# Summing over partitions in squares: attention denominators by VectorE's transposes instead of TensorE's products with ones

## The chip, the cores and the metric

The kernel runs on one core of a Trainium2 chip. A core has TensorE (PE: matrix products, from SBUF into PSUM), VectorE (DVE), ScalarE (ACT), GpSimd (POOL) and DMA queues; each engine works through its own instructions in order and waits for the others by semaphores. The metric is device time in microseconds, the median of several runs; less is better. Before the change it is 3609.92 us (three runs, 3609.66 to 3611.45).

## The reference

Four images of 64x64 pixels with 256 channels, float32. Two layers, one after the other.

```python
# layer 0: attention of every pixel over all 4096 pixels of its image
q = x @ Wq + bq ; k = x @ Wk + bk ; v = x @ Wv + bv       # 32, 32 and 256 wide
attn = softmax(q k^T, axis=-1)
x = gamma * (attn @ v) + x
# layer 1: 3x3 depthwise convolution to 768, two pointwise layers, local attention
hid = gelu(conv3x3(x) @ w_up1 + b_up1)                    # 512 wide
h = x + hid @ w_up2 + b_up2
q, k, v = split(h @ w_qkv + b_qkv)
w = softmax(q . k over the 3x3 window / 16)               # zero-padded borders
out = h + sum over the window of w * v
```

Both softmaxes are computed without a shift: exponentials are summed, and the result is multiplied by the reciprocal of the sum. The change is about these two sums, the denominators.

## The kernel before

An image is cut into 8 blocks of 512 pixels, so there are 32 slots, one for each block. Slot s does the attention of layer 0 for block s and, interleaved with it, the stages of layer 1 for earlier blocks: `hidden`, `update`, `guide` and `scores` for block s-3, `local_product` for block s-5. A slot has 16 points. At each point TensorE gets an energy (every second point), one job of the list, and a `product` that adds to the accumulators `acc`:

```python
jobs = [
    job(hidden, k, 0) + job(hidden, k, 1), job(local_denominator, a),
    job(hidden, k, 2), job(local_product, a, 0), job(hidden, k, 3),
    ...  # cut: update, guide, scores, local_sum (point 12), local_values (13 and 14)
]
...  # cut
    for point in range(points):
        G, half = divmod(point, 2)
        after = slot + (G + 1) // NG, (G + 1) % NG
        if half == 0:
            if G == NG // 2 and slot + 1 < NSLOT:
                spread_queries(slot + 1)

            if G == NG // 2:
                for do in job(border, k - 1):
                    do()
            if after[0] < NSLOT:
                energy(*after)
        if after[0] < NSLOT:
            weight(*after, half)
        for do in jobs[point]:
            do()
        product(slot, G, half)

        if point == 0:
            add_up(slot, 0, 0)
        if point < points - 1:
            add_up(slot, *divmod(point + 1, 2))

        while stepped < min(n_steps, -(-(point + 1) * n_steps // (points - 2))):
            next(conv, None)
            stepped += 1
    ...  # cut: loads
...
if slot < NSLOT - 1:
    next(finish(slot))
```

The exponentials `p` have keys on the 128 partitions and pixels (queries) on 512 columns. VectorE adds them up in `den`; what is left is a sum over partitions:

```python
def add_up(s, G, half):

    p = weights[s, G, half]
    if G == 0 and half == 0:
        sums[s] = tile_of([P, 2, NB], "den", f"den_{s}")
        nc.vector.tensor_copy(sums[s], p)
        return
    den = sums[s]
    nc.vector.tensor_tensor(den, den, p, ALU.add)
    if G == NG - 1 and half == 1:
        nc.vector.tensor_tensor(den[:, 0, :], den[:, 0, :], den[:, 1, :], ALU.add)
```

`finish` sums `den` over partitions by a product with a matrix of ones. Where there is a local denominator `lsums[a]` of an earlier block (slots 4 to 30, "shared"), the two are summed side by side in halves of 64 columns of the array; one reciprocal serves both, and copies spread the halves over 128 partitions:

```python
def finish(s, parts=((0, RB),)):

    g = s % NBLK
    den, acc = sums.pop(s), accs.pop(s)

    dps = bank("m", f"dps_{s}")
    rden = tile_of([P, NB], "rden", f"rden_{s}", 2)
    a = s - LAG_ATT + 1


    shared = 0 <= a < DIRECT - 1
    if shared:
        for half, weights_ in zip(halves, (den[:, 0, :], lsums.pop(a))):
            nc.tensor.matmul(
                dps[half], lhsT=ones[:, : P // 2], rhs=weights_, start=True, stop=True
            )
        lrdens[a] = tile_of([P, CH, NB], "xc", f"turned_{s}", 2)[:, 0, :]
    else:
        nc.tensor.matmul(dps, lhsT=ones, rhs=den[:, 0, :], start=True, stop=True)
    os = [tile_of([P, NB], "o", f"o_{s}_{c}", 3) for c in range(CH)]
    for r0, r1 in parts:
        n = slice(r0 * W, r1 * W)
        nc.vector.reciprocal((lrdens[a] if shared else rden)[:, n], dps[:, n])
        if shared:
            for half in halves:
                nc.vector.tensor_copy(rden[half], lrdens[a][halves[0]])
        for c, o in enumerate(os):
            nc.vector.scalar_tensor_tensor(
                o[:, n], acc[c][:, n], gam[:, 0:1], rden[:, n], ALU.mult, ALU.mult
            )
        for c, o in enumerate(os):
            dst = xv[:, c, 1 + g * RB + r0 : 1 + g * RB + r1, 1 : 1 + W]
            nc.vector.tensor_tensor(
                dst, o[:, n].rearrange("p (h w) -> p h w", w=W), dst, ALU.add
            )
        if r1 < RB:
            yield
    watch(den[:, 0, :])
    if len(parts) > 1:
        yield
    watch(rden)
    for o in os:
        watch(o)
    yield

def local_denominator(s):
    turned, lrdens[s] = lrdens[s], tile_of([P, NB], "rden", f"lrden_{s}", 2)
    for half in halves:
        nc.scalar.copy(lrdens[s][half], turned[halves[1]])
    watch(lrdens[s])
```

The local denominator's tile is summed by GpSimd, and in the last blocks by TensorE directly:

```python
def local_sum(s):


    t = tile_of([P, NB], "lsum", f"lsum_{s}")
    tv = t.rearrange("p (h w) -> p h w", w=W)
    nc.gpsimd.memset(t, 0.0)
    for half in range(2):
        for (block, t_), rows, of in pieces(s):
            to = tv[:, rows, columns(half)]
            nc.gpsimd.tensor_tensor(to, to, near_ws[block, half][:, t_, of, :], ALU.add)
    one = t[0:1, :].rearrange("p (h w) -> p h w", w=W)
    edge = one[:, :, 0 : W : W - 1]
    nc.gpsimd.tensor_tensor(edge, edge, pad_side[0:1], ALU.add)
    row = edge_row(s)
    if row is not None:
        nc.gpsimd.tensor_tensor(one[:, row, :], one[:, row, :], pad_line[0:1], ALU.add)
    watch(t)
    lsums[s] = t
...  # cut
def local_reciprocal(s):
    lrdens[s] = tile_of([P, NB], "rden", f"lrden_{s}", 2)
    nc.vector.reciprocal(lrdens[s], totals.pop(s))
    watch(lrdens[s])
```

`watch(values)` adds a tile into `watched` on GpSimd, so that at the end an overflow can be seen (`good`, `bad`); a second, shifted version of the whole kernel then runs. It does not run with these inputs. PSUM has 8 banks: 4 for the energies `e`, 2 for `acc`, 2 under the name "m" for all jobs and for `dps`.

Of the kernel before, what the change touches and what calls it, by code (L numbers as in the profile page):

```python
# [9 lines left out]
F32 = mybir.dt.float32  # L10
AF = mybir.ActivationFunctionType
ALU = mybir.AluOpType
AX = mybir.AxisListType
PSUM = bass.MemoryType.PSUM

P = 128
B, H, W, C = 4, 64, 64, 256
N = H * W
CQK = C // 8
CH = C // P  # L20
HP, WP = H + 2, W + 2
NB = 512
RB = NB // W
# [12 lines left out]
NEG = -1.0e30  # L36
GRP = P // CQK
NG = NT // GRP
NSLOT = B * NBLK


# [3 lines left out]
LAG_PERC, LAG_HID, LAG_ATT = 2, 3, 5  # L45
# [3 lines left out]
def attention_then_perception_kernel(  # L49
# [19 lines left out]
    nc = tc.nc  # L69

    const = ctx.enter_context(tc.tile_pool(name="const", bufs=1))
# [4 lines left out]
        return t  # L76

    ones = const.tile([P, P], F32, tag="ones", name="ones")
    watched = const.tile([P, NB], F32, tag="watched", name="watched")
    bad = const.tile([P, 1], mybir.dt.int32, tag="bad", name="bad")  # L80


# [1 line left out]
    def unshifted():  # L84
# [6 lines left out]
        def tile_of(shape, tag, name, bufs=1):  # L91
            return pool.tile(shape, F32, tag=tag, name=name, bufs=bufs)

        def bank(tag, name):
            return psum.tile([P, NB], F32, tag=tag, name=name, bufs=2)
# [46 lines left out]
        for r in range(KR):  # L142
            m = near[r * KW : (r + 1) * KW]
# [9 lines left out]
                if abs(q - 1 - r) > 1:  # L153
                    nc.gpsimd.memset(m[:, :, q, :], 0.0)

        ident = pool.tile([P, P], F32, tag="ident", name="ident")
        make_identity(nc, ident)

        def watch(values):

            nc.gpsimd.tensor_tensor(watched, watched, values, ALU.add)  # L161


        queries, keys, values, staged = {}, {}, {}, {}
# [94 lines left out]


        energies, weights, sums, accs, lsums, lrdens = {}, {}, {}, {}, {}, {}
        halves = slice(0, P // 2), slice(P // 2, P)

        DIRECT = NSLOT - LAG_HID - 1

# [31 lines left out]
        def add_up(s, G, half):  # L297
# [8 lines left out]
            if G == NG - 1 and half == 1:  # L306
                nc.vector.tensor_tensor(den[:, 0, :], den[:, 0, :], den[:, 1, :], ALU.add)  # L307

        def finish(s, parts=((0, RB),)):

            g = s % NBLK
            den, acc = sums.pop(s), accs.pop(s)

            dps = bank("m", f"dps_{s}")
            rden = tile_of([P, NB], "rden", f"rden_{s}", 2)
            a = s - LAG_ATT + 1


            shared = 0 <= a < DIRECT - 1
            if shared:  # L320
                for half, weights_ in zip(halves, (den[:, 0, :], lsums.pop(a))):
                    nc.tensor.matmul(  # L322
                        dps[half], lhsT=ones[:, : P // 2], rhs=weights_, start=True, stop=True
                    )
                lrdens[a] = tile_of([P, CH, NB], "xc", f"turned_{s}", 2)[:, 0, :]
            else:
                nc.tensor.matmul(dps, lhsT=ones, rhs=den[:, 0, :], start=True, stop=True)
            os = [tile_of([P, NB], "o", f"o_{s}_{c}", 3) for c in range(CH)]
            for r0, r1 in parts:
                n = slice(r0 * W, r1 * W)  # L330
                nc.vector.reciprocal((lrdens[a] if shared else rden)[:, n], dps[:, n])  # L331
                if shared:
                    for half in halves:
                        nc.vector.tensor_copy(rden[half], lrdens[a][halves[0]])
                for c, o in enumerate(os):
                    nc.vector.scalar_tensor_tensor(
                        o[:, n], acc[c][:, n], gam[:, 0:1], rden[:, n], ALU.mult, ALU.mult
                    )
                for c, o in enumerate(os):
                    dst = xv[:, c, 1 + g * RB + r0 : 1 + g * RB + r1, 1 : 1 + W]  # L340
                    nc.vector.tensor_tensor(
                        dst, o[:, n].rearrange("p (h w) -> p h w", w=W), dst, ALU.add
                    )
                if r1 < RB:
                    yield
            watch(den[:, 0, :])
            if len(parts) > 1:
                yield
            watch(rden)
            for o in os:  # L350
                watch(o)
            yield

        def local_denominator(s):
            turned, lrdens[s] = lrdens[s], tile_of([P, NB], "rden", f"lrden_{s}", 2)
            for half in halves:
                nc.scalar.copy(lrdens[s][half], turned[halves[1]])
            watch(lrdens[s])


        percs, hids, hs = {}, {}, {}
# [219 lines left out]
        def local_values(s, t):  # L581
            ps = job_bank(f"lv_{s}_{t}")
            for half in range(2):
                for kin in range(CH):
                    nc.tensor.matmul(  # L585
                        ps[:, half * C : (half + 1) * C],
                        lhsT=keys_of(s, t, half, kin), rhs=wlv[:, kin, :],
                        start=(kin == 0), stop=(kin == CH - 1),
                    )
            for half in range(2):  # L590
                if s < NSLOT - 2:
                    lvs[s, t, half] = tile_of([P, C], "lv", f"lv_{s}_{t}_{half}", 8)
                else:
                    if not half:
                        late[s, t] = tile_of([P, NB], "perc", f"lv_{s}_{t}", NPERC)
                    lvs[s, t, half] = late[s, t][:, half * C : (half + 1) * C]
                lv = lvs[s, t, half]
                nc.vector.tensor_tensor(lv, ps[:, half * C : (half + 1) * C], blv, ALU.add)  # L598
                if s >= NSLOT - 1:

                    square = tile_of([P, 2, NB], "den", f"lv_{s}_{t}_{half}_2")[:, 0, :C]
                    nc.gpsimd.tensor_tensor(square, lv, lv, ALU.mult)
                    nc.gpsimd.tensor_tensor(watched[:, :C], watched[:, :C], square, ALU.add)

        def pieces(s):

# [9 lines left out]
        def scores(s, half):  # L616


            g = s % NBLK
            ps = job_bank(f"s_{s}_{half}")  # L620

            tiles, rows, top = (2, QR, 0) if s < NSLOT else (1, UP, RB)
            n = tiles * rows * QW
            for t in range(tiles):
                for kin in range(CH):
                    nc.tensor.matmul(  # L626
                        ps[:, t * QR * QW : t * QR * QW + rows * QW].rearrange(
                            "p (h w) -> p h w", w=QW
                        ),
                        lhsT=keys_of(s, t, half, kin),  # L630
                        rhs=guides[0][:, kin, top + t * KR : top + t * KR + rows, columns(half)],
                        start=(kin == 0), stop=(kin == CH - 1),
                    )
            if s < NSLOT - 2:
                p = tile_of([P, 2 * QR * QW], f"lp{half}", f"lp_{s}_{half}", 2)
            else:

                if s < NSLOT:
                    late[s] = tile_of([P, NB], "perc", f"lp_{s}_{half}", NPERC)
                elif not half:  # L640
                    late[s] = tile_of([P, NB], "lsum", f"lp_{s}")
                p = late[s][:, : 2 * QR * QW]
                if s == NSLOT:
                    p = late[s][:, half * C : half * C + QR * QW]
            near_ws[s, half] = p.rearrange("p (t h w) -> p t h w", h=QR, w=QW)
            nc.scalar.activation(p[:, :n], ps[:, :n], AF.Exp, scale=C**-0.5)  # L646
            engine = nc.vector if s >= NSLOT - 2 else nc.gpsimd
            pv = p[:, :n].rearrange("p (t n) -> p t n", t=tiles)
            mask = near[:, half, :rows, :].rearrange("p h w -> p (h w)")
            engine.tensor_tensor(  # L650
                pv, pv, mask.unsqueeze(1).to_broadcast([P, tiles, rows * QW]), ALU.mult
            )

            if g == 0:
                nc.gpsimd.memset(p[P // 2 :, : UP * QW], 0.0)
                if s < NSLOT:
                    nc.gpsimd.memset(p[: P // 2, UP * QW : QR * QW], 0.0)
            if s >= DIRECT:

                nc.gpsimd.tensor_tensor(watched[:, :n], watched[:, :n], p[:, :n], ALU.add)  # L660

        def local_sum(s):

# [11 lines left out]
            row = edge_row(s)  # L675
            if row is not None:
                nc.gpsimd.tensor_tensor(one[:, row, :], one[:, row, :], pad_line[0:1], ALU.add)
            watch(t)
            lsums[s] = t

        def local_total(s):
# [18 lines left out]
                )  # L700

        def local_reciprocal(s):
            lrdens[s] = tile_of([P, NB], "rden", f"lrden_{s}", 2)
            nc.vector.reciprocal(lrdens[s], totals.pop(s))  # L704
            watch(lrdens[s])

        def local_product(s, c):
            b, g = divmod(s, NBLK)
# [58 lines left out]
        for slot in range(NSLOT):  # L767
# [44 lines left out]
            for point in range(points):  # L812
# [18 lines left out]
                    add_up(slot, 0, 0)  # L831
                if point < points - 1:
                    add_up(slot, *divmod(point + 1, 2))

                while stepped < min(n_steps, -(-(point + 1) * n_steps // (points - 2))):
                    next(conv, None)
# [481 lines left out]
```

## Time and profile before

| | |
|---|---|
| time | 3609.92 us (3609.66 to 3611.45) |
| span of the profiled execution | 3607.3 us |
| TensorE busy | 3579.5 us, 99% |
| VectorE busy | 2377.5 us, 66% |
| ScalarE busy | 1145.5 us, 32% |
| GpSimd busy | 705.9 us, 20% |
| granted TensorE clock, mean | 0.998 |

A page of the profile lists the busy time of each engine, the chain of work that ended last, and the costliest groups of instructions. A line of a group reads: source line, engine, operation, the tiles written and read, shapes, count, then busy time, the mean duration of one in ns, and the idle time of the engine before it with what ended it. A float32 product appears as two records, one for each pass; durations of products overlap, because they are pipelined, so starts tell more than durations. A line of a timeline has the start, the time taken by the merged instructions, the engine, the source line and the operation; a bracket gives the idle time before it and what released it.

The operations that the change removes or makes smaller, by group:

| operation | count | busy us | mean ns |
|---|---|---|---|
| VectorE reciprocal of 128x512 (shared) | 27 | 90.7 | 3358 |
| VectorE reciprocal of 128x512 (slots 0 to 3) | 4 | 13.4 | 3358 |
| VectorE reciprocal of 128x512 (local, last blocks) | 5 | 16.8 | 3354 |
| VectorE copy of 64x512 | 54 | 22.7 | 420 |
| ScalarE copy of 64x512 | 54 | 33.3 | 616 |
| GpSimd watch of den | 32 | 40.6 | 1268 |
| GpSimd watch of rden | 32 | 40.7 | 1273 |
| GpSimd watch of lrden | 32 | 50.3 | 1572 |
| GpSimd watch of lsum | 28 | 36.9 | 1319 |

### The profile page before, as it was taken

How to read it: one execution, taken by the hardware profiler on the slowest of the kernel's cores; microseconds unless marked ns; L12 is line 12 of the kernel's file. 1: busy time of each engine (PE TensorE's matmuls, PEld its weight loads, DVE VectorE, ACT ScalarE, POOL GpSimd, SP SyncE). 2: the span in 40 equal slices, each digit the busy share in tenths (PEclk: the TensorE clock that was granted, in tenths of full speed). 3: DMA queues.
4: the chain of work that ended last, by engine and by line, in shares of the span. 5: the costliest groups of instructions: out<-in, count | busy, mean ns of one | idle time of the engine just before them, and what ended most of it. 6: DMA issues, size and time to landing. Idle time of an engine off the chain costs nothing.

```text
span 3607.3 us, 29497 instructions
## 1 busy us (share of the span) xinstructions
PE 3579.5 (99%) x11400; PEld 1696.9 (47%) x11400; DVE 2377.5 (66%) x2742; ACT 1145.5 (32%) x1324; POOL 705.9 (20%) x720
## 2 busy tenths in 40 slices
PE   9999999999999999999999999999999999999998
PEld 4444444454444444455444444444544444444445
DVE  3376676657666667765666666675667766666976
ACT  2223333323333333332333333333233333333431
POOL 1010112111221222121112222112112122221224
PEclk9999999999999999999999999999999999999999
DMA  3000000010000000011000000001100000000000
GB/s 104 6 3 4 0 9 15 23 39 21 15 7 9 15 15 15 21 24 44 15 15 15 3 12 15 15 21 35 33 15 15 15 15 3 12 15 15 6 6 25
DMA packets 84532, 64.68 MB, mean 18 GB/s; under 512 B 57280, under 2 KB 62528, under 8 KB 84256
## 3 DMA queue, kind: packets, MB, share of 16 engines
q1 hardware_dynamic: 83568, 62.19, 5.9%
q8 instruction: 91, 1.49, 0.2%
q10 hardware_dynamic: 816, 0.53, 0.0%
q14 instruction: 57, 0.47, 0.0%
HBM read 41.52 MB, written 18.81 MB: 17 GB/s over the span
## 4 chain that ended last, share of the span: by engine, by line
PE 97%; DVE 3%; issue 0%; ACT 0%; DMA 0%; POOL 0%; SPq 0%; ACTq 0%; DVEq 0%
PE acc L291 48%; PE hid L424 18%; PE e L272 7%; PE dx L450 6%; PE v L235 3%; PE lv L585 3%; PE g L533 3%; PE lo L713 2%; PE s L626 2%; DVE perc L397 2%; PE qk L201 1%; PE dps L322 1%; PE c L565 0%; DVE den L305 0%; DVE rden L331 0%; DVE lrden L704 0%
## 5 line engine op out<-in xcount | busy, mean ns | idle before, releaser
L291 PE MATMUL acc<-p,v 128*128 128x512 f32 x4096 | 1837.4, 595 | 0.1
L397 DVE SCALAR_TENSOR_TENSOR perc<-xp,wperc,perc 128x512 f32<-128x512 f32 (+1 forms) x1554 | 1298.0, 836 | 430.2 <-ACT perc L393 395.0
L291 PEld LDWEIGHTS acc<-p,v 128*128 128x128 f32 x4096 | 769.5, 190 | 917.8 <-issue 913.9
L280 ACT ACTIVATE p<-e 128x1024 f32<-128x1024 f32 x512 | 524.3, 1024 | 1469.8 <-PE e L272 832.0
L424 PE MATMUL hid<-perc,wup 128*128 128x512 f32 x1536 | 686.1, 599 | 1.0 <-DVE perc L397 1.0
L305 DVE TENSOR_TENSOR den<-den,p 128x1024 f32<-128x1024 f32 x480 | 604.1, 1259 | 44.3 <-ACT p L280 40.6
L424 PEld LDWEIGHTS hid<-perc,wup 128*128 128x128 f32 x1536 | 284.7, 190 | 390.5 <-issue 377.6
L272 PE MATMUL e<-qa,ka 32*128 32x512 f32 x2048 | 291.9, 640 | 0.0
L161 POOL TENSOR_TENSOR watched<-watched,lo 128x512 f32<-128x512 f32 x62 | 127.1, 2049 | 670.5 <-DVE lo L720 670.3
L450 PE MATMUL dx<-hid,wup 128*128 128x512 f32 x512 | 233.0, 598 | 0.0
L428 ACT ACTIVATE hid<-hid,bup 128x512 f32<-128x512 f32 x128 | 88.0, 687 | 436.7 <-PE hid L424 436.7
L650 POOL TENSOR_TENSOR lp<-lp,near 128x396 f32<-128x396 f32 x60 | 57.8, 963 | 715.9 <-ACT lp L646 715.9
L598 DVE TENSOR_TENSOR lv<-lv,blv 128x256 f32<-128x256 f32 x130 | 49.1, 419 | 193.6 <-PE lv L585 193.6
L331 DVE RECIPROCAL turned<-dps 128x512 f32<-128x512 f32 x27 | 90.7, 3358 | 128.2 <-PE dps L322 128.2
L272 PEld LDWEIGHTS e<-qa,ka 32*128 32x128 f32 x2048 | 80.0, 182 | 171.7 <-issue 168.4
L456 DVE SCALAR_TENSOR_TENSOR h<-dx,bup,xp 128x256 f32<-128x256 f32 x128 | 56.0, 479 | 158.7 <-PE dx L450 158.7
L450 PEld LDWEIGHTS dx<-hid,wup 128*128 128x128 f32 x512 | 94.6, 190 | 129.9 <-issue 123.2
L393 ACT ACTIVATE perc<-xp,bperc,wperc 128x512 f32<-128x512 f32 x192 | 153.8, 803 | 5.2 <-PE hid L424 5.2
L280 ACT ACT_TABLE_LOAD x91 | 116.8, 1283 | 120.0 <-issue 119.4
L585 PE MATMUL lv<-wlv,h 128*128 128x256 f32 x520 | 126.5, 385 | 1.6 <-DVE lv L598 0.9
L161 POOL TENSOR_TENSOR watched<-watched,den 128x512 f32<-128x512 f32 x32 | 40.6, 1268 | 431.4 <-DVE den L307 431.4
L235 PE MATMUL v<-wv,xc 128*128 128x256 f32 x512 | 118.4, 384 | 6.1 <-DMA wv<-in_w_v 5.3
(105 smaller groups left out, 2064.0 us busy)
## 6 DMA issues: line engine op xcount, KB each, us to landing
xp<-in_x SPq DMA_DIRECT2D x30, 528.0 KB, 4.0
out<-lo SPq DMA_DIRECT2D x58, 256.0 KB, 2.0
xc<-in_x SPq DMA_DIRECT2D x48, 256.0 KB, 3.3
qa<-packed SPq DMA_DIRECT2D x124, 64.0 KB, 2.0
ka<-st SPq DMA_DIRECT2D x124, 16.0 KB, 1.8
packed<-st SPq DMA_DIRECT2D x31, 64.0 KB, 1.9
wup<-in_w_up SPq DMA_DIRECT2D x1, 1536.0 KB, 7.1
out<-res SPq DMA_DIRECT2D x6, 256.0 KB, 2.0
```

The costliest lines, as they stand in the source:

```text
L161: nc.gpsimd.tensor_tensor(watched, watched, values, ALU.add)
L235: nc.tensor.matmul(ps[:, i * C : (i + 1) * C], lhsT=xc[:, kin, bass.ts(2 * pair + i, P)], rhs=wv[:, kin, :], start=(kin == 0), stop=(kin = ...
L272: nc.tensor.matmul(e[:, j, :], lhsT=key[rows, :], rhs=queries[s][rows, :], start=True, stop=True,)
L280: nc.scalar.activation(p, energies[s, G][:, 2 * half : 2 * half + 2, :], AF.Exp)
L291: nc.tensor.matmul(accs[s][c], lhsT=v[:, 2 * half + i, bass.ts(c, P)], rhs=p[:, i, :], start=(first and i == 0), stop=(G == NG - 1 and hal ...
L305: nc.vector.tensor_tensor(den, den, p, ALU.add)
L393: nc.scalar.activation(acc, win, AF.Identity, bias=bperc[:, half, j : j + 1], scale=wt)
L397: nc.vector.scalar_tensor_tensor(acc, win, wt, acc, ALU.mult, ALU.add)
L424: nc.tensor.matmul(ps, lhsT=wup1[:, i, bass.ts(d, P)], rhs=percs[s][i], start=(i == 0), stop=(i == NPC - 1),)
L450: nc.tensor.matmul(ps, lhsT=wup2[:, d, bass.ts(c, P)], rhs=hids[s][:, d, :], start=(d == 0), stop=(d == NHC - 1),)
L533: nc.tensor.matmul(ps, lhsT=wg[:, kin, bass.ts(i, P)], rhs=pixels(s, kin), start=(kin == 0), stop=(kin == CH - 1),)
L585: nc.tensor.matmul(ps[:, half * C : (half + 1) * C], lhsT=keys_of(s, t, half, kin), rhs=wlv[:, kin, :], start=(kin == 0), stop=(kin == CH ...
```

## The change

The sum over 128 partitions is split in two steps. VectorE transposes each 32x32 square of the 128x512 tile, so that pixels come to lie on partitions within a square, and sums each square's 32 columns: 16 columns are left, with four groups of 32 partitions still to be added. TensorE adds these with the matrix `fold` (ones where two partitions agree modulo 32) in one product of 16 columns, or 32 for two denominators. The reciprocal is then taken of 16 or 32 columns; a spreading copy and another transpose of squares bring it back to 512 columns on all partitions. The aim is to take the sums off TensorE and to shorten the reciprocals.

The squares are summed at the slot's last point (`partial_sums`), before `finish`. The copies for the local denominator go from ScalarE to VectorE. `watched` has 256 columns, longer tiles are added in pieces, and the small tiles are watched in place of the large ones.

```diff
@@ -36,6 +36,8 @@
 NEG = -1.0e30
 GRP = P // CQK
 NG = NT // GRP
+SQ = 32
+NJ = NB // SQ
 NSLOT = B * NBLK
 
 
@@ -76,7 +78,7 @@
         return t
 
     ones = const.tile([P, P], F32, tag="ones", name="ones")
-    watched = const.tile([P, NB], F32, tag="watched", name="watched")
+    watched = const.tile([P, C], F32, tag="watched", name="watched")
     bad = const.tile([P, 1], mybir.dt.int32, tag="bad", name="bad")
 
 
@@ -153,12 +155,25 @@
                 if abs(q - 1 - r) > 1:
                     nc.gpsimd.memset(m[:, :, q, :], 0.0)
 
-        ident = pool.tile([P, P], F32, tag="ident", name="ident")
+        ident = tile_of([P, NB], "lsum", "ident")[:, :P]
         make_identity(nc, ident)
 
+
+        fold = pool.tile([P, P], F32, tag="fold", name="fold")
+        nc.gpsimd.memset(fold, 0.0)
+        for q in range(0, P, SQ):
+            part = fold[q : q + SQ].rearrange("p (j r) -> p j r", r=SQ)
+            nc.gpsimd.affine_select(
+                out=part, in_=part, compare_op=ALU.not_equal, fill=1.0,
+                base=0, pattern=[[0, P // SQ], [-1, SQ]], channel_multiplier=1,
+            )
+
         def watch(values):
 
-            nc.gpsimd.tensor_tensor(watched, watched, values, ALU.add)
+            n = values.free_size()
+            for i in range(0, n, C):
+                at = watched[:, : min(C, n - i)]
+                nc.gpsimd.tensor_tensor(at, at, values[:, i : min(n, i + C)], ALU.add)
 
 
         queries, keys, values, staged = {}, {}, {}, {}
@@ -259,7 +274,7 @@
 
 
         energies, weights, sums, accs, lsums, lrdens = {}, {}, {}, {}, {}, {}
-        halves = slice(0, P // 2), slice(P // 2, P)
+        parts_, inverses, turneds = {}, {}, {}
 
         DIRECT = NSLOT - LAG_HID - 1
 
@@ -306,32 +321,53 @@
             if G == NG - 1 and half == 1:
                 nc.vector.tensor_tensor(den[:, 0, :], den[:, 0, :], den[:, 1, :], ALU.add)
 
+        def squares(t):
+            return t.rearrange("p (j r) -> p j r", r=SQ)
+
+        def shared(s):
+
+            a = s - LAG_ATT + 1
+            return a if 0 <= a < DIRECT - 1 else None
+
+        def partial_sums(s):
+
+
+            a = shared(s)
+            parts_[s] = tile_of([P, 2, NJ], "parts", f"parts_{s}")
+            turneds[s] = tile_of([P, CH, NB], "xc", f"turned_{s}", 2)
+            todo = [sums[s][:, 0, :]] + ([] if a is None else [lsums.pop(a)])
+            for i, t in enumerate(todo):
+                nc.vector.transpose(turneds[s][:, i, :], t)
+                nc.vector.tensor_reduce(
+                    parts_[s][:, i, :], squares(turneds[s][:, i, :]), axis=AX.X, op=ALU.add
+                )
+            watch(parts_[s][:, : len(todo), :].rearrange("p i j -> p (i j)"))
+
+        def on_all(values, turned, out):
+
+            nc.vector.tensor_copy(
+                squares(turned), values.unsqueeze(2).to_broadcast([P, NJ, SQ])
+            )
+            nc.vector.transpose(out, turned)
+
         def finish(s, parts=((0, RB),)):
 
             g = s % NBLK
-            den, acc = sums.pop(s), accs.pop(s)
-
-            dps = bank("m", f"dps_{s}")
+            acc = accs.pop(s)
+            n = NJ * (1 if shared(s) is None else 2)
+            ps = bank("m", f"dps_{s}")[:, :n]
+            given = parts_.pop(s).rearrange("p i j -> p (i j)")[:, :n]
+            nc.tensor.matmul(ps, lhsT=fold, rhs=given, start=True, stop=True)
+            inverse = tile_of([P, 2, NJ], "inverse", f"inverse_{s}")
+            inverses[s] = inverse
+            nc.vector.reciprocal(inverse.rearrange("p i j -> p (i j)")[:, :n], ps)
             rden = tile_of([P, NB], "rden", f"rden_{s}", 2)
-            a = s - LAG_ATT + 1
-
-
-            shared = 0 <= a < DIRECT - 1
-            if shared:
-                for half, weights_ in zip(halves, (den[:, 0, :], lsums.pop(a))):
-                    nc.tensor.matmul(
-                        dps[half], lhsT=ones[:, : P // 2], rhs=weights_, start=True, stop=True
-                    )
-                lrdens[a] = tile_of([P, CH, NB], "xc", f"turned_{s}", 2)[:, 0, :]
-            else:
-                nc.tensor.matmul(dps, lhsT=ones, rhs=den[:, 0, :], start=True, stop=True)
+            on_all(inverse[:, 0, :], turneds[s][:, 0, :], rden)
+            watch(inverse.rearrange("p i j -> p (i j)")[:, :n])
+            sums.pop(s)
             os = [tile_of([P, NB], "o", f"o_{s}_{c}", 3) for c in range(CH)]
             for r0, r1 in parts:
                 n = slice(r0 * W, r1 * W)
-                nc.vector.reciprocal((lrdens[a] if shared else rden)[:, n], dps[:, n])
-                if shared:
-                    for half in halves:
-                        nc.vector.tensor_copy(rden[half], lrdens[a][halves[0]])
                 for c, o in enumerate(os):
                     nc.vector.scalar_tensor_tensor(
                         o[:, n], acc[c][:, n], gam[:, 0:1], rden[:, n], ALU.mult, ALU.mult
@@ -341,21 +377,16 @@
                     nc.vector.tensor_tensor(
                         dst, o[:, n].rearrange("p (h w) -> p h w", w=W), dst, ALU.add
                     )
-                if r1 < RB:
+                if len(parts) > 1:
                     yield
-            watch(den[:, 0, :])
-            if len(parts) > 1:
-                yield
-            watch(rden)
             for o in os:
                 watch(o)
             yield
 
         def local_denominator(s):
-            turned, lrdens[s] = lrdens[s], tile_of([P, NB], "rden", f"lrden_{s}", 2)
-            for half in halves:
-                nc.scalar.copy(lrdens[s][half], turned[halves[1]])
-            watch(lrdens[s])
+            at = s + LAG_ATT - 1
+            lrdens[s] = tile_of([P, NB], "rden", f"lrden_{s}", 2)
+            on_all(inverses[at][:, 1, :], turneds[at][:, 1, :], lrdens[s])
 
 
         percs, hids, hs = {}, {}, {}
@@ -600,7 +631,7 @@
 
                     square = tile_of([P, 2, NB], "den", f"lv_{s}_{t}_{half}_2")[:, 0, :C]
                     nc.gpsimd.tensor_tensor(square, lv, lv, ALU.mult)
-                    nc.gpsimd.tensor_tensor(watched[:, :C], watched[:, :C], square, ALU.add)
+                    watch(square)
 
         def pieces(s):
 
@@ -657,7 +688,7 @@
                     nc.gpsimd.memset(p[: P // 2, UP * QW : QR * QW], 0.0)
             if s >= DIRECT:
 
-                nc.gpsimd.tensor_tensor(watched[:, :n], watched[:, :n], p[:, :n], ALU.add)
+                watch(p[:, :n])
 
         def local_sum(s):
 
@@ -675,7 +706,6 @@
             row = edge_row(s)
             if row is not None:
                 nc.gpsimd.tensor_tensor(one[:, row, :], one[:, row, :], pad_line[0:1], ALU.add)
-            watch(t)
             lsums[s] = t
 
         def local_total(s):
@@ -700,9 +730,13 @@
                 )
 
         def local_reciprocal(s):
+            inverse = tile_of([P, 2, NJ], "inverse", f"linverse_{s}")[:, 0, :]
+            turned = tile_of([P, NB], "st", f"lturned_{s}")
+            nc.vector.transpose(turned, totals.pop(s))
+            nc.vector.reciprocal(inverse, squares(turned)[:, :, 0])
             lrdens[s] = tile_of([P, NB], "rden", f"lrden_{s}", 2)
-            nc.vector.reciprocal(lrdens[s], totals.pop(s))
-            watch(lrdens[s])
+            on_all(inverse, turned, lrdens[s])
+            watch(inverse)
 
         def local_product(s, c):
             b, g = divmod(s, NBLK)
@@ -831,6 +865,8 @@
                     add_up(slot, 0, 0)
                 if point < points - 1:
                     add_up(slot, *divmod(point + 1, 2))
+                else:
+                    partial_sums(slot)
 
                 while stepped < min(n_steps, -(-(point + 1) * n_steps // (points - 2))):
                     next(conv, None)
```

## The prediction

> **What bounds the kernel now.** I read the page first: busy times, then the chain that ended last.
>
> ```profile
> PE 3579.5 (99%) x11400; PEld 1696.9 (47%) x11400; DVE 2377.5 (66%) x2742; ACT 1145.5 (32%) x1324; POOL 705.9 (20%) x720
> ...
> PE 97%; DVE 3%; issue 0%; ACT 0%; DMA 0%; POOL 0%; SPq 0%; ACTq 0%; DVEq 0%
> ```
>
> TensorE is busy for 99% of the span and is 97% of the chain. The stretches of 200 us between 200 and 3400 us each show 200.00 us of PE. So work taken from another engine is worth nothing there, and every microsecond taken from TensorE's in-order queue is worth a microsecond, unless a wait takes its place. The list of groups with shapes kept apart then says what the change can take:
>
> ```profile
> L322 PE MATMUL dps<-lsum,ones 128*64 128x512 f32 x54 | 28.9, 618 | 0.0
> L322 PE MATMUL dps<-den,ones 128*64 128x512 f32 x54 | 28.9, 618 | 0.0
> ...
> L327 PE MATMUL dps<-den,ones 128*128 128x512 f32 x10 | 5.1, 592 | 0.0
> ```
>
> Each float32 product is two records (passes). 27 slots (4 to 30) sum the two denominators side by side, 28.9 us in all (the two lines overlap); five slots (0 to 3 and 31) sum one, 5.1 us. About 34 us of 3610 is the ceiling of the main effect, 0.9%. What one slot boundary looks like is in the timeline around 1917 us (slot 15 to 16):
>
> ```profile
> 1904.67 1.27 POOL L161 TENSOR_TENSOR watched<-watched,lsum 128x512 f32<-128x512 f32 x1
> ...
> 1912.81 0.69 DVE L307 TENSOR_TENSOR den<-den 128x512 f32<-128x512 f32 x1
> ...
> 1917.65 0.64 PE L322 MATMUL dps<-den,ones 128*64 128x512 f32 x1
> ...
> 1918.13 0.59 PE L322 MATMUL dps<-den,ones 128*64 128x512 f32 x1
> ...
> 1918.66 1.14 PE L272 MATMUL e<-qa,ka 32*128 32x512 f32 x8
> ...
> 1918.80 3.36 DVE L331 RECIPROCAL turned<-dps 128x512 f32<-128x512 f32 x1 [5.30 <-PE dps L322]
> ...
> 1919.73 10.57 PE L424 MATMUL hid<-perc,wup 128*128 128x512 f32 x24
> ```
>
> Columns: start, duration, engine, line, operation. Three things are to be seen. The denominator is complete at 1912.81 + 0.69 = 1913.50, and TensorE asks for it at 1917.65: 4.15 us of slack (the first shared boundary, at 462 us, has the same). lsum is complete at 1904.67, long before. And the 3.36 us reciprocal hides under e and hid (11.6 us), so its shortening gains nothing in these slots.
>
> **What the Trainium skill says.** "VectorE: DVE Perf Modes", section "The three transpose paths", says that VectorE transposes only within 32x32 blocks, and gives 311 ns for 128x128 bf16; the trace of before holds no such transpose. "TensorE: Matmul & The Clock Gate", section "LDWEIGHTS (loading the stationary operand)", makes the weight load depend on the columns loaded and not on the rows or on the moving operand: 128 columns / 1.2 = 107 ns. The trace agrees: four passes of the 128x128 weight turnings take 0.42 us of loads, 0.105 each. So a product of 16 columns costs its weight loads, not its columns. "TensorEngine Tiling (Array Packing)", section "Key Properties", says that changing the tiling mode drains the engine; the trace agrees, as acc's passes are 0.43 us apart, but from acc's last pass to a product on another tiling 0.52 us. "TensorE: Matmul & The Clock Gate", section "Part 1: The HAM clock gate (the "warmup" mystery)", says that idleness halves the clock; below, at 118 us, passes are 0.86 us apart after a gap.
>
> **The change part by part.**
>
> Shared slots, TensorE. Now: a tiling switch of 0.09 (0.52 less 0.43), then 1.01 us from dps to e (1918.66 less 1917.65, which includes 0.09 for the switch to e). Gone: 1.10. New: one product with 128x128 weights and 32 columns, two passes. The nearest measured thing is the product of 16 columns on 128x128 weights in the tail:
>
> ```profile
> 3505.55 0.32 PE L697 MATMUL ld<-pad,ones 128*128 128x16 f32 x2
> 3505.80 0.35 PE L565 MATMUL c<-h,small 128*1 128x8 f32 x8
> ```
>
> Start to start 0.25 us for its two passes. With the switch to e (0.09) the new boundary costs 0.34. Gain 1.10 - 0.34 = 0.76 us, times 27: 20.5 us.
>
> Slots 0 to 3. dps to e takes 0.95 (at 112.67 us: 113.62 less 112.67); new 0.34; gain 0.61 each, 2.4 us.
>
> VectorE before the product. Two transposes and two reductions now come after den. A transpose of 512 columns, estimated from the skill's 311 ns: that is 128/0.96 = 133 ns plus 178 fixed, so 512/0.96 + 178 = 0.71 us (the skill's clock of 0.96 GHz, section "Specifications"). A reduction of 128x512 took 0.67 us (good, in the tail). Sum 2 x (0.71 + 0.67) = 2.8 us, against 4.15 of slack: it fits with 1.3 us to spare, and no wait arises. Where the next image's projections lie ahead of dps, the slack is about 3.5 us more.
>
> VectorE after it. Gone: 3.36 + 0.85 us. New: reciprocal of 32 columns (0.56 us for 64 and 2.94 for 448 give 6.2 ns a column and 0.16 fixed: 0.36), a spreading copy (0.4 to 0.7) and a transpose 0.71: some 1.6. acc is free 2.6 us earlier, which TensorE doesn't need. ScalarE's two copies (1.24 us) become a copy and a transpose on VectorE, 1.3 us. VectorE's sum per shared slot: -4.2 + 2.8 + 1.6 + 1.3 = +1.5 us in 106, nothing at 66% load. GpSimd loses most watching of den, rden, lrden and lsum, 168.5 us of 706: off the path.
>
> The start. In slots 1 and 2 there is no hid to hide the reciprocal:
>
> ```profile
> 114.69 0.66 PE L485 MATMUL wq_turning<-ident,wq_in 128*128 128x128 f32 x4
> ...
> 117.14 0.66 PE L485 MATMUL wk_turning<-ident,wk_in 128*128 128x128 f32 x4 [1.79 <-DVE rden L331]
> ...
> 117.93 8.83 PE L291 MATMUL acc<-p,v 128*128 128x512 f32 x16
> ```
>
> TensorE waits 1.79 us for the bank that the reciprocal holds, then runs acc's first four passes at half clock (8.83 us instead of 7.06). The reciprocal of 16 columns frees the bank before it is asked for. acc is then the wait: 0.26 + 0.6 + 0.7 and two scalings of 0.7 after the product give 2.7 us after it, against 2.4 of TensorE's own work. So of 1.79 + 0.13 + 1.77 = 3.7 us some 3 go if the clock stays up, and 1.5 if it doesn't: 2.5. At slot 2 (188 us) a wait of 0.46 goes and the half clock perhaps: 0.8.
>
> The tail. Here VectorE is on the chain:
>
> ```profile
> 3541.34 6.28 PE L424 MATMUL hid<-perc,wup 128*128 128x512 f32 x14 [1.03 <-DVE perc L397]
> ```
>
> Its row of taps begins after the last finish, where reciprocals of 0.56 + 2.94 us become one of 0.26 and 1.3 of spreading: taps start some 2.4 us sooner. Two masks between them wait for ScalarE (exp done at 3528.7, mask now at 3530.03), so about 1.7 us reach hid, dps's 0.61 included. At the very end two 3.36 us reciprocals lie on the chain:
>
> ```profile
> 3592.37 3.36 DVE L704 RECIPROCAL lrden<-ld 128x512 f32<-128x512 f32 x1 [1.94 <-PE ld L697]
> ```
>
> Each becomes transpose 0.7, reciprocal 0.26, copy 0.5, transpose 0.7: about 2.1, so 1.2 sooner. Both, and half a column count in the last reduction: 2.5 us.
>
> Sum: 20.5 + 2.4 + 2.5 + 0.8 + 1.7 + 2.5 = 30.4; 3609.9 - 30.4 = 3579.5, say 3580.
>
> **The rivals.**
>
> 1. The product waits for VectorE. For it: den is the last thing VectorE makes in a slot, and four dependent operations are put behind it. Against it: 4.15 us of slack. If a float32 transpose took two cycles a column (1.25 us), the four would take 3.8 us, which still just fits. With 1.7 us each (4.7 us in all) TensorE would wait 0.6 us per slot: 16 us back, about 3596.
> 2. The small product isn't small. If the second weight load, and e's, each stood bare (0.19 us each instead of 0.105, plus a drain of 0.17), the boundary would cost 0.7 and not 0.34: a gain of 0.4 in 27 slots, 11 us, about 3591.
> 3. The staging buffers. The transposed tile shares two buffers with the input blocks of the next image. Before, ScalarE's last read ended at 693.55 us, the load landed about 3.1 us after its issue, and the product over it began at 698.04. VectorE's read comes after four taps (end 692.4), so 693.7: at most some tenths, three times. About 3581.
> 4. Nothing is gained, because another engine sets the pace of a slot. Against it: no other engine has 70% busy, and TensorE has no gap to fill. It would leave 3610.
>
> **Range and chances.** The large term rests on TensorE's occupation and on one cost (0.25 us, which could be 0.15 to 0.6); the small terms (7.5 us) may halve or double. Better everywhere gives 3572; rival 2, or half of rival 1 with weaker ends, gives 3590. So 3580, and 3571 to 3590. Two per cent would need 3538, more than twice the whole of dps, or 3682, a new wait of over 2 us at every boundary: chances 0.01 and 0.02.
>
> **What would show it.** In the changed profile: the fold product two records of some 0.25 us start to start, beginning right behind acc without an idle time put down to VectorE's reductions; from acc's last pass to e about 0.8 us where it was 1.5; a slot near 105.8 us instead of 106.5; transposes near 0.71 us; no wait at 117 us and no half clock after it; the last lrden about 2.1 us long. A wait of the fold product for "parts", a slower transpose, or stalls in hid at slots 7, 15 and 23 would make it wrong.

## The result

The changed kernel takes 3572.64 us (five runs, 3571.6 to 3573.02) where the kernel before took 3609.92: ratio 0.9896, 95% interval 0.9881 to 0.9910. That is 37.3 us less; the prediction was 3580 (3571 to 3590).

### The profile after

The head of the page, and its chain:

```profile
PE 3548.8 (99%) x11346; PEld 1701.1 (48%) x11346; DVE 2320.2 (65%) x2938; ACT 1113.0 (31%) x1270; POOL 612.6 (17%) x804
...
PE 97%; DVE 2%; issue 0%; ACT 0%; DMA 0%; SPq 0%; ACTq 0%; DVEq 0%
```

TensorE is as full as before, over a shorter span (3571.3 against 3607.3 us). The timeline of the same slot boundary that the prediction showed (counted from 0 it is slot 17 to 18, not 15 to 16):

```profile
1890.06 7.03 PE L306 MATMUL acc<-p,v 128*128 128x512 f32 x16
...
1892.18 0.69 DVE L322 TENSOR_TENSOR den<-den 128x512 f32<-128x512 f32 x1
1892.91 0.71 DVE L340 STREAM_TRANSPOSE turned<-den 128x512 f32<-128x512 f32 x1
1893.65 0.69 DVE L341 TENSOR_REDUCE parts<-turned 128x16 f32<-128x512 f32 x1
...
1894.99 0.69 DVE L341 TENSOR_REDUCE parts<-turned 128x16 f32<-128x512 f32 x1
...
1896.93 0.30 PE L360 MATMUL dps<-parts,fold 128*128 128x32 f32 x2
1897.16 1.14 PE L287 MATMUL e<-qa,ka 32*128 32x512 f32 x8
1897.27 0.36 DVE L363 RECIPROCAL inverse<-dps 128x32 f32<-128x32 f32 x1 [1.59 <-PE dps L360]
```

The fold product starts where acc's passes end (1890.06 + 16 x 0.43) and e starts 0.23 us later. The sums are ready at 1895.68, 1.25 us before TensorE wants them, and no idle time stands before the fold product.

### Where the 36 us of span went

TensorE's starts in the two traces, compared at dps (or the fold product) and at the energies e behind it:

| stretch | span gained, us | of it the product itself | prediction |
|---|---|---|---|
| up to the end of slot 0 | 0.56 | 0 | 0 |
| boundaries 0 to 3 and the slots between | 8.79 | 4 x 0.73 = 2.9 | 2.4 + 3.3 |
| slots 4 to 30, 27 boundaries | 23.43 | 27 x 0.87 | 20.5 |
| slot 31, up to its own product | 0.22 | 0 | 0 |
| last product to the last local products | 0.63 | 0.72 | 1.7 |
| the end | 2.57 | 0 | 2.5 |
| sum | 36.20 | | 30.4 |

The rows are differences of starts, added up to the last product of the program, which starts 36.20 us sooner (3600.41 and 3564.21); the spans differ by 36.0 and the times of the two profiled runs, 3609.61 and 3573.02, by 36.6. The first row is the loading of weights and not the change: the first products start a little sooner, and among the profiled runs of the variants below the product at the end of slot 0 starts anywhere from 111.99 to 113.88 us.

### The profile page after: what moved, and what is told of

Its sections match the earlier page's. It is cut to its first block, busy times and chain, and to the rows that moved or that the text cites. A ratio compares the mean times of both kernels' runs of the same rounds, so it can differ in the third digit from the quotient of the medians.

```text
span 3571.3 us, 29494 instructions
## 1 busy us (share of the span) xinstructions
PE 3548.8 (99%) x11346; PEld 1701.1 (48%) x11346; DVE 2320.2 (65%) x2938; ACT 1113.0 (31%) x1270; POOL 612.6 (17%) x804
## 3 DMA queue, kind: packets, MB, share of 16 engines
q8 instruction: 91, 1.49, 0.2%
## 4 chain that ended last, share of the span: by engine, by line
PE 97%; DVE 2%; issue 0%; ACT 0%; DMA 0%; SPq 0%; ACTq 0%; DVEq 0%
PE acc L306 49%; PE hid L455 19%; PE e L287 8%; PE dx L481 6%; PE v L250 3%; PE lv L616 3%; PE g L564 3%; PE lo L747 3%; PE s L657 3%; DVE perc L428 2%; PE qk L216 1%; PE c L596 0%; DVE den L320 0%; PE ld L727 0%; PE dps L360 0%
## 5 line engine op out<-in xcount | busy, mean ns | idle before, releaser
L428 DVE SCALAR_TENSOR_TENSOR perc<-xp,wperc,perc 128x512 f32<-128x512 f32 (+1 forms) x1554 | 1257.5, 810 | 525.9 <-ACT perc L424 490.7
L320 DVE TENSOR_TENSOR den<-den,p 128x1024 f32<-128x1024 f32 x480 | 594.8, 1239 | 42.8 <-ACT p L295 39.2
L176 POOL TENSOR_TENSOR watched<-watched,lo 128x256 f32<-128x256 f32 x124 | 157.0, 1266 | 999.0 <-DVE lo L754 994.0
L176 POOL TENSOR_TENSOR watched<-watched,o 128x256 f32<-128x256 f32 x128 | 124.0, 969 | 56.2 <-DVE o L372 48.6
L564 PE MATMUL g<-h,wg 128*128 128x512 f32 x256 | 123.1, 604 | 0.0
```

The source lines that it names most:

```text
L176: nc.gpsimd.tensor_tensor(at, at, values[:, i : min(n, i + C)], ALU.add)
L428: nc.vector.scalar_tensor_tensor(acc, win, wt, acc, ALU.mult, ALU.add)
L564: nc.tensor.matmul(ps, lhsT=wg[:, kin, bass.ts(i, P)], rhs=pixels(s, kin), start=(kin == 0), stop=(kin == CH - 1),)
```

## The experiments

All variants are of the changed kernel.

**1. The old products put back.** Does TensorE's occupied time make the gain, or VectorE's shorter chain?

```diff
             todo = [sums[s][:, 0, :]] + ([] if a is None else [lsums.pop(a)])
+            if a is not None:
+                pairs[s] = todo
 ...  # cut
-            ps = bank("m", f"dps_{s}")[:, :n]
+            full = bank("m", f"dps_{s}")
+            ps = full[:, :n]
+            if s in pairs:
+                for half, weights_ in zip(halves, pairs.pop(s)):
+                    nc.tensor.matmul(
+                        full[half], lhsT=ones[:, : P // 2], rhs=weights_, start=True, stop=True
+                    )
             given = parts_.pop(s).rearrange("p i j -> p (i j)")[:, :n]
             nc.tensor.matmul(ps, lhsT=fold, rhs=given, start=True, stop=True)
```

> The changed kernel, with the two old products of 512 columns (den and lsum with ones) put back ahead of the fold product in the 27 shared slots; their result is overwritten. Theory (TensorE's occupied time at the boundary is the gain): 0.09 us for the switch to 64 columns, 0.86 of passes and up to 0.2 for the loads behind it come back, about 1.0 to 1.2 us in each of 27 slots: 3600 to 3605 us. Rival (the shorter reciprocal and VectorE's shorter chain are the gain): nothing of VectorE's work changes, so 3573.

Measured 3604.27 us (3603.33 to 3604.88), ratio to before 0.9985 (0.9978 to 0.9991): 31.6 us come back. In its timeline the pair starts 0.09 us later behind acc than the fold product did and takes 1.01 us up to the fold product, which then takes 0.34 instead of 0.23: 1.21 us in each of the 27 slots, 32.6 us. (In the tail of this trace the clock stays high, which gives some of it back; see below.)

```profile
1913.86 0.64 PE L365 MATMUL dps<-den,ones 128*64 128x512 f32 x1
...
1914.87 0.41 PE L369 MATMUL dps<-parts,fold 128*128 128x32 f32 x2
1915.21 1.14 PE L288 MATMUL e<-qa,ka 32*128 32x512 f32 x8
```

A shared slot now takes 106.87 us from e to e, where the kernel before takes 106.53 and the changed one 105.66. So VectorE's new chain, with the short reciprocals, gives nothing in these slots as long as the pair is there. The rival falls.

**2. The sums made twice.** How much delay do the steps before the product bear?

```diff
-            for i, t in enumerate(todo):
+            for i, t in list(enumerate(todo)) * (2 if a is not None else 1):
```

> The changed kernel, with the two transposes and two reductions before the fold product made twice in the shared slots (2.8 us more). Theory: the slack between the last reduction and the fold product is 1.25 us (3 slots before an image's end have some 3.5 us more), so TensorE waits 1.5 us in 24 slots: about 3609 us, nothing left of the gain, and the fold product is named as waiting for the reductions. Rival (VectorE's 65% leaves room, its sums cost nothing): 3573.

Measured 3611.88 us (3608.23 to 3612.54), ratio to before 1.0002 (0.9993 to 1.0011): the gain is gone. The same boundary in its timeline:

```profile
1918.30 0.69 DVE L341 TENSOR_REDUCE parts<-turned 128x16 f32<-128x512 f32 x1
1919.04 0.41 PE L360 MATMUL dps<-parts,fold 128*128 128x32 f32 x2 [1.32 <-DVE parts L341]
```

The bracket is what to look for: TensorE idle for 1.32 us until VectorE's reduction. The list of waits has it 24 times (31.8 us in all): in every shared slot but the three that end with the next image's projections. The slot grew by 1.59 us: the product starts 1.92 us after acc's last pass instead of 0.43, and takes 0.33 us to e instead of 0.23. Behind the first of the 24 waits the granted clock was 0.50 for 3.41 us (from 457.22), which cost 1.7 us more; behind the other 23 it stayed at 1.00.

**3. One transpose more.**

```diff
-                nc.vector.transpose(turneds[s][:, i, :], t)
+                for _ in range(2 if a is not None and i == 0 else 1):
+                    nc.vector.transpose(turneds[s][:, i, :], t)
```

> The changed kernel, with one transpose more (0.73 us) before the fold product in the shared slots. Theory of 1.25 us slack: 3573 us, no wait. If the true slack (with the signal to TensorE) is under 0.7 us: up to 0.7 x 24, at most 3590.

Measured 3572.03 us (3571.71 to 3572.74), no change. So the slack ends between 0.7 and 2.8 us of additions. Variant 2 narrows it down: 2.8 us of additions delayed the product by 1.49 us, which leaves 1.3, in line with the 1.25 us of the timeline.

**4. A long reciprocal in the shared slots.**

```diff
+            if shared(s) is not None:
+                nc.vector.reciprocal(rden, sums[s][:, 0, :])
             on_all(inverse[:, 0, :], turneds[s][:, 0, :], rden)
```

> The changed kernel, with a reciprocal of 512 columns (3.36 us) put back on VectorE behind the small one in the shared slots; its result is overwritten. Theory: it hides under energies and hid (11.6 us of TensorE), so 3573 us, within 1 us. Rival (shorter reciprocals are the gain in the slots): up to 27 x 3.4 = 91 us more, 3664.

Measured 3572.02 us (3570.37 to 3573.38), no change: 27 reciprocals of 3.36 us, 91 us of VectorE's work on the chain that frees acc, cost nothing under 11.6 us of energies and hid.

**5. The same in slots 0 to 2 alone** (`if s < 3`).

> The changed kernel, with a reciprocal of 512 columns (3.36 us) put back on VectorE behind the small one in slots 0 to 2 only; its result is overwritten. Theory (in slots 1 and 2 no hid hides VectorE's chain, and the gap halves TensorE's clock): acc waits about 3.2 us at slot 1 and 0.8 at slot 2, and up to 1.8 and 1.4 us of half clock follow: 3577 to 3580 us. Rival (the 5.9 us won at these two boundaries beyond the product itself are a matter of chance in the start of the run): 3573.

Measured 3578.34 us (3577.85 to 3580.35), 5.7 more. Its timeline at slot 1:

```profile
114.39 3.29 DVE L366 RECIPROCAL rden<-den 128x512 f32<-128x512 f32 x1
...
119.55 4.97 PE L306 MATMUL acc<-p,v 128*128 128x512 f32 x7 [3.28 <-DVE o L374]
```

TensorE waits 3.28 us for acc, and seven passes then take 4.97 us, where seven at 0.43 take 3.0: the granted clock is 0.50 for 3.41 us from 119.72, and again from 191.41 in slot 2, as in the kernel before. Start by start, slot 1 loses 4.7 us and slot 2 2.4; the third reciprocal costs nothing. So two reciprocals in the right place weigh more than 27 elsewhere.

**6. No product at all.** If the rest of the product is TensorE's, VectorE can add the four groups too:

```diff
+            for q in range(P // SQ):
+                nc.vector.tensor_copy(four[:, q, :n], flat[q * SQ : (q + 1) * SQ, :n])
 ...  # cut
-            nc.tensor.matmul(ps, lhsT=fold, rhs=given, start=True, stop=True)
 ...  # cut
-            nc.vector.reciprocal(inverse.rearrange("p i j -> p (i j)")[:, :n], ps)
 ...  # cut
+            nc.vector.tensor_reduce(
+                total[:, :n], fours.pop(s)[:, :, :n].rearrange("p q n -> p n q"), axis=AX.X, op=ALU.add
+            )
+            nc.vector.reciprocal(flat[:SQ, :n], total[:, :n])
+            for q in range(1, P // SQ):
+                nc.vector.tensor_copy(flat[q * SQ : (q + 1) * SQ, :n], flat[:SQ, :n])
```

> The changed kernel without any product for the denominators: VectorE copies the four groups of 32 partitions side by side (four small copies), adds them by one reduction, takes the reciprocal on 32 partitions and copies it to the other three groups. Theory: TensorE loses the 0.23 us from fold product to e, but the switch to e (0.09), which the fold product covered, comes back: 0.14 us in 32 slots, 4.5 us, and the wait of 0.25 us at slot 1 goes: 3568. Rival 1 (the fold product's 0.23 us is all its own): 3565. Rival 2 (the small copies bring a wait on VectorE): 3573 or more.

Measured 3566.32 us (3565.86 to 3566.7), ratio to before 0.9881 (0.9866 to 0.9896): 6.3 us below the changed kernel, and every run of it below every run of that one. Its timeline:

```profile
1887.14 7.03 PE L306 MATMUL acc<-p,v 128*128 128x512 f32 x16
...
1892.79 0.72 DVE L350 COPY four<-parts 32x32 f32<-32x32 f32 x4
...
1893.55 0.36 DVE L369 TENSOR_REDUCE total<-four 32x32 f32<-32x128 f32 x1
1893.94 0.34 DVE L372 RECIPROCAL inverse<-total 32x32 f32<-32x32 f32 x1
1894.10 1.14 PE L287 MATMUL e<-qa,ka 32*128 32x512 f32 x8
```

From acc's last pass to e there are now 0.09 us (1887.14 + 16 x 0.43 is 1894.02), so the product cost 0.14 beyond the switch; over 32 boundaries that is 4.5 us. Half a microsecond more is won at slot 1, where the wait of 0.25 us is gone. In the two traces a further 1.3 us lie in the tail, and they are not the product's: there the granted clock is 0.50 for 3.41 us, and in the changed kernel's trace for 6.83 (shown below). VectorE's busy time rose from 2320.2 to 2368.1 us, and no wait of TensorE's shows it.

**7. The old overflow sums back on GpSimd** (den, rden, lrden, lsum).

```diff
-            sums.pop(s)
+            watch(rden)
+            watch(sums.pop(s)[:, 0, :])
 ...  # cut
+            watch(lrdens[s])
 ...  # cut
+            watch(t)
             lsums[s] = t
```

> The changed kernel, with the overflow sums of den, rden, lrden and lsum put back on GpSimd (512 columns each, in two pieces). Theory (GpSimd is off the path): 3573 us, within 1 us, with GpSimd 150 to 200 us busier; if GpSimd slows VectorE where both read SBUF, VectorE's taps go back from 816 ns towards the 843 ns of before without moving the time. Rival (GpSimd's relief is part of the gain): up to some 5 us slower.

Measured 3574.24 us (3573.83 to 3574.41), 1.6 more than the changed kernel: more than the 1 us expected. GpSimd is busy for 871.8 us.

**8. The sums of o and lo left out**, so that the check for overflow is incomplete.

> The changed kernel, which leaves out the overflow sums of o and lo (281 us of GpSimd's work; the check for overflow is then incomplete). Theory: time 3573 us, unchanged; if GpSimd slows VectorE, the mean of the taps (816 ns) and of the additions to den (1239 ns) falls further.

A single run, 3569.67 us; its span is 3.4 us shorter than the changed kernel's. It was expected to stay; the difference is larger than the 1.4 us over which five runs of the changed kernel spread. The taps in the groups of the changed kernel, of variant 7 and of variant 8 (busy, mean of one in ns, idle before):

```profile
L428 DVE SCALAR_TENSOR_TENSOR perc<-xp,wperc,perc 128x512 f32<-128x512 f32 x1518 | 1237.7, 816 | 524.8 <-ACT perc L424 490.7
```

```profile
L430 DVE SCALAR_TENSOR_TENSOR perc<-xp,wperc,perc 128x512 f32<-128x512 f32 x1518 | 1275.1, 841 | 498.4 <-ACT perc L426 464.3
```

```profile
L426 DVE SCALAR_TENSOR_TENSOR perc<-xp,wperc,perc 128x512 f32<-128x512 f32 x1518 | 1198.7, 790 | 587.1 <-ACT perc L422 553.0
```

The same 1518 instructions take 790, 816 or 841 ns on average as GpSimd is busy for 363, 613 or 872 us (843 and 706 in the kernel before). In slots 4 to 30 that changes no start but those of the three slots that load the next image. In slot 31, which has 97 taps where others have 48, VectorE is late for TensorE; changed kernel and variant 7:

```profile
3370.71 1.99 PE L616 MATMUL lv<-wlv,h 128*128 128x256 f32 x8 [0.68 <-DVE lv L629]
```

```profile
3372.58 1.99 PE L618 MATMUL lv<-wlv,h 128*128 128x256 f32 x8 [1.52 <-DVE lv L631]
```

The wait goes from 0.68 to 1.52 us, and in variant 8 no such wait is listed. Start by start, variant 7 loses 0.23 us in each of the three slots that load the next image, 0.84 at this wait and 0.89 in the first hid behind the last product, which waits 0.62 us for taps. It gets 1.3 back in the tail, where the clock is low for 3.41 us and not for 6.83. Variant 8 gains 1.4 us in slot 31, and 1.3 from that same clock: so less than half of its 3.4 us can be put down to GpSimd.

## Why the prediction was right, and where its terms were off

**Right: the bound and the mechanism.** TensorE's order sets the time, the sums by ones are what is gained, and the long reciprocal is hidden in the steady slots. Variants 1 and 4 show both. The slack was predicted as 1.3 us and measured as 1.25; the transposes at 0.71 us each, which they take to the hundredth. The Trainium skill's 311 ns for 128 columns of bf16 ("VectorE: DVE Perf Modes", "The three transpose paths"), scaled by columns as an estimate, fits float32 here too: 711 ns. All terms together came out 5.8 us too small, so that the time lies where the prediction put "better everywhere", 3572, though not every term was better.

**Too small: the shared boundary**, 0.76 predicted, 0.87 measured, 3 us in 27. The term "0.25 for two passes plus 0.09 for the switch to e" counted the switch twice: the 0.25 had been read between starts in the tail, from a small product to one on another tiling, and held it already. Acc's end to e is 0.23 with the product and 0.09 without (variant 6); in slot 31, where a product on the same tiling follows, the fold product takes 0.14. The reading of weight loads beside it was off too: "0.105 each" divides the 0.42 us in which four overlapping loads of 0.14 us ran, and most loads of 128 columns in that trace last 0.19 us. The sum did not use it. That columns hardly count came out: with 16 columns the product takes 0.22 us to e, with 32 it takes 0.23.

**Too small: the start**, 3.3 predicted (2.5 + 0.8), 5.9 measured. The half clock went at both slots, where the prediction counted two thirds of it at the first and a quarter at the second. Timeline of the changed kernel at slot 1:

```profile
113.90 0.60 PE L516 MATMUL wk_turning<-ident,wk_in 128*128 128x128 f32 x4
...
114.75 7.13 PE L306 MATMUL acc<-p,v 128*128 128x512 f32 x16 [0.25 <-DVE o L372]
```

No wait stands before wk_turning, and acc's 16 passes take 7.13 us, not 8.83; at slot 2 they run at 0.43 too. The busy times of a stretch give the granted clock directly, as the third number from the end; before (where it is 0.50 from 189.69 too) and after:

```profile
118.01:121.42 3.41, 3.41 (x4) 1.39 (x5) 3.41 (x5) 0.00 (x0) 3.25 (x3) 0.50 0.00 0
```

```profile
118.01:121.42 3.41, 3.41 (x10) 1.37 (x8) 3.20 (x4) 1.02 (x1) 0.63 (x1) 1.00 0.00 0
```

The prediction's wait for acc, 0.3 us, is there with 0.25. Variant 5 brings the wait and the slow passes back together.

**Too large: the last finish**, 1.7 predicted (0.6 of it the product), 0.63 measured (0.72 of it the product). The step "taps start some 2.4 us sooner" failed: against TensorE's own products they start as before. ScalarE, in the changed kernel:

```profile
3460.28 0.69 ACT L459 ACTIVATE hid<-hid,bup 128x512 f32<-128x512 f32 x1 [3.35 <-PE hid L455]
3460.87 1.51 ACT L424 ACTIVATE perc<-xp,bperc,wperc 128x512 f32<-128x512 f32 x2
```

xp was complete at 3459.77, but the first tap is ScalarE's, and in its queue it stands behind the gelu of hid, which waits for TensorE. VectorE's idle time before the taps grew from 1.05 to 1.94 us instead. This rests on the trace; no variant moved the instruction.

Yet what the step was to bring about did happen: the last six taps take 6.37 us in place of 8.19, and the wait of hid for them, 1.03 us before, is gone. TensorE's clock took it back. In the tail it is low before the change too, but for half as long; before and after:

```profile
3534.75:3538.16 3.41, 3.41 (x5) 1.35 (x5) 3.34 (x3) 1.04 (x1) 3.33 (x3) 0.50 0.00 0
```

```profile
3499.25:3506.08 6.83, 6.50 (x18) 3.35 (x19) 6.65 (x8) 1.55 (x2) 6.10 (x7) 0.50 0.00 0
```

The stretch from ld (3495.71) to lo (3513.82) takes 18.1 us in both kernels. In the traces of variants 2, 5, 6, 7 and 8, whose clock is low there for 3.41 us, it takes 16.7 to 16.8; in those of variants 3 and 4, with 6.83 us, 18.1 and 18.3; in that of variant 1, whose clock stays high there, 16.3. So 1.3 us of gain are hidden in this trace, and with them the term would have been about 1.9. What decides how long the clock stays low, the runs don't show.

**Right: the end**, 2.5 predicted, 2.57 measured: the last lrden takes 2.28 us from the transpose of ld to its own end, where it took 3.36. This too is read from the traces alone.

**The rivals.** A wait for VectorE did not arise, and variant 2 shows what it would have cost. The product is small. The staging buffers cost nothing: the loads at the image's end are issued at 681.53 us, 4.56 before the product over them, where it was 4.46 before. "Another engine sets the pace" holds only at the start, in slot 31 and in the tail.

## What to carry to other kernels

When one engine fills 99% of the span, price a change by the starts on that engine on both sides of what is removed, and take a measured interval between starts for what it is: it includes the switch to the next shape. Then ask of each step put ahead of that engine how long before its use the input was ready: here 1.25 us were left, and doubling the steps lost the whole gain. The same instruction is worth nothing where the bound engine has other work and much where it has none, and there a wait of 1.8 us cost about as much again through the clock; and if the other engine can finish the job alone, as in variant 6, even the last small product is worth removing.

## What was not expected of the hardware

VectorE's instructions lengthen while GpSimd works: taps of 128x512 take 790 to 841 ns on average with 363 to 872 us of GpSimd. Taken one by one, the taps with no GpSimd instruction beside them last 737 to 754 ns in the traces of both kernels and of variants 7 and 8; the 158 to 352 (of 1518) with one beside them last 1123 to 1269 on average. The addition of o into xp, which runs just as GpSimd sums o, took 1224 ns before, 1032 after, and 686 when GpSimd's sums of o and lo were left out. That is why VectorE's busy time fell by 57 us although the change gives it more instructions (2938 against 2742), which by themselves take 24 us more (171 for 147). Why they interfere, the runs don't show.

A product of 32 columns behind acc's passes costs TensorE 0.14 us beyond the switch. From its start to e it takes 0.23 us there, but 0.33 behind a wait (variant 2) and 0.34 behind the pair of products on another tiling (variant 1).
